# A four-layer convolution and scan kernel: the WKV layer's backward pass reordered and partly moved to PSUM, and the zero frames of layer 0 written in other shapes

## The chip, the core and the metric

The kernel runs on one core of one Trainium2 chip, as a single program of four layers. The metric is the device time of one execution in microseconds (us): the median of three runs. A profile of one further execution, with the hardware profiler, gives the times of single instructions. The engines are PE (TensorE: matrix products), DVE (VectorE), ACT (ScalarE), POOL (GpSimd) and SP, which here only issues DMAs. SBUF is the on-chip memory, PSUM the small memory with eight banks that PE writes its products to, and a DMA moves data between these and the DRAM.

## The reference

The input x has shape [2, 192, 96, 96]: two images, 192 channels, 9216 positions. Each layer normalizes its input and adds its result to it. Two of the four layers bear on the change.

Layer 0 is a convolution with learned offsets. A 1x1 product reduces 192 channels to 180 and another makes offsets; values are then gathered around each position with bilinear weights, and a position outside the image counts as zero.

Layer 2 is the WKV recurrence, over the 9216 positions in order, for each channel by itself. It has three products, k, v and r, of the normalized input, and then, as the reference writes it:

```
no = max(o, u + k);  A = exp(o - no);  B = exp(u + k - no)
y  = (A*p + B*v) / (A*q + B)
no2 = max(w + o, k); A2 = exp(w + o - no2); B2 = exp(k - no2)
p, q, o = A2*p + B2*v,  A2*q + B2,  no2
```

The recurrence runs over the positions in both directions, and the mean of the two results is taken; the kernel brings both quotients over one denominator, in which the sigmoid of r enters as a factor 1 + exp(-r). The product of mean and sigmoid is then normalized over the channels, multiplied by the matrix w_o and added to x.

## The kernel before, in words

**Layer 0.** DRAM holds two frames per image: xp_d, the reduced image with a border of zeros (PITCH = 106 rows and columns, of CW = 194 values), and o_d, the offsets, with zero rows ahead and behind. Before the reduce stage a tile of zeros is set by one DVE memset (L250), and six DMAs per image on ACT's queue write the borders (L256 to L273): two for o_d in 97 lanes, two for the full rows of xp_d in 106 lanes, two for its side strips in 96 lanes. A lane is one partition of the zero tile. The reduce stage (`reduce0`) then loads 128 positions at a time on SP's queue (L283), normalizes them on DVE (xn, L114), multiplies on PE (L300) and writes both frames through a tile xk (L294). Its tiles take memory that the zero tile had, so they wait for the zero DMAs to finish.

**Layer 2.** The two images' 192 channels each are packed in three groups g of 128 lanes: g = 0 and 1 hold the first 128 channels of each image, g = 2 the 64 that remain of both. The positions are cut into 18 chunks of 512. The loop runs over 54 chunk-groups forward and then over 54 backward. In this layer PE, ACT, DVE and POOL each execute in the order in which the program text issues (`manual_schedule`), so the order of the calls in the loop is the schedule. DMAs are issued by SP ahead of it.

An iteration i works on several chunk-groups at once:

- `key(i+3)`: matmuls for k into PSUM (L1607, two buffers).
- `carry(i+2)`: ACT copies the three columns in which the scans start from the previous tile of this group (L1708).
- `top(i+2)`: a DVE scan for the running maximum (L1719), and z = k minus it (L1728).
- `weighted(i+1)`: ACT makes four weights of z, each by Relu (L1734) and Exp (L1736).
- `times_v(i+1)` and `own(i)`: POOL multiplies weights by v (L1751, L1777).
- `value(i+2)` (forward): matmuls for v and an ACT copy with bias (L1685). `gate(i+1)` (backward): matmuls for r into the same PSUM buffer, and on ACT Relu (L1693) and Exp (L1694) into er, in SBUF with two buffers.
- `sums(i)`: two DVE scans (L1758) and two products (L1772) for numerator and denominator.
- `ended(i)`: two POOL sums (L1782, L1783). Forward, the result goes to DRAM as half_d; backward it is loaded again.
- Backward alone: `crossed(i-1)` (POOL, L1790) and `joined(i-1)` combine the two directions: three DVE operations (L1794, L1795, L1796, the last multiplying by 1 + er), a POOL sum (L1799), and on ACT Ln and Exp (L1801, L1802), which approximate an inverse r0. `inverse(i-2)` (POOL, L1807) and `scaled(i-2)` (DVE, L1814, L1817) do one Newton step and make h.

When the three groups of a chunk are done, a `tail` starts. It is a generator that is advanced twice per iteration: PE subtracts the channel mean (L1558, 16 matmuls), ACT squares (L1831), PE sums the squares (L1838), ACT takes the inverse root by Ln and Exp (L1840, L1841), DVE and POOL refine it by a Newton step (L1845, L1846, L1848), PE spreads it (L1852, `turn`), DVE multiplies h (L1853), PE multiplies by w_o (L1860, L1863) for each of two halves m, and DVE adds bias and input (L1873) and takes statistics (L1881). Two tails can be under way at once.

Of the kernel before, what the change touches and what calls it, by code (L numbers as in the profile page):

```python
# [61 lines left out]
class Net:  # L62
# [130 lines left out]
    def reduce_constants(self, wn, xp_d, o_d):  # L193
# [5 lines left out]
        with tc.tile_pool(name="wr0", bufs=1) as wr, tc.tile_pool(  # L199
# [49 lines left out]
            zero = wr.tile([PITCH, 8 * NS], F32, name="zero")  # L249
# [3 lines left out]
            for b in range(B):  # L253

                for lo, n in ((0, 2 * OB), (HW, OB + OA)):
                    nc.scalar.dma_start(  # L256
                        out=o_d[b][lo : lo + n].rearrange("(p r) c -> p (r c)", p=97),
                        in_=zero[:97, : n // 97 * 2 * NS],
                    )
                for lo, hi in ((0, F), (F + H, PITCH)):  # L260
                    rows = xp_d[b][lo:hi].rearrange("y x c -> (y x c)")
                    nc.scalar.dma_start(
                        out=rows.rearrange("(p f) -> p f", p=PITCH),
                        in_=zero[:, : (hi - lo) * CW],
                    )
                nc.scalar.dma_start(
                    out=xp_d[b][F : F + H, :F, :].rearrange("y x c -> y (x c)"),
                    in_=zero[:H, : F * CW],
                )
                nc.scalar.dma_start(  # L270
                    out=xp_d[b][F : F + H, F + W :, :].rearrange("y x c -> y (x c)"),
                    in_=zero[:H, : end * CW],
                )  # L273
# [1214 lines left out]
    def layer2(self, x, out, stats):  # L1488
# [10 lines left out]
        with ExitStack() as ctx:  # L1499
# [5 lines left out]
            pk = ctx.enter_context(tc.tile_pool(name="l2k", bufs=2, space=PSUM))  # L1505
            pv = ctx.enter_context(tc.tile_pool(name="l2v", bufs=1, space=PSUM))
            pa = ctx.enter_context(tc.tile_pool(name="l2a", bufs=2, space=PSUM))
            pm = ctx.enter_context(tc.tile_pool(name="l2m", bufs=3, space=PSUM))
# [29 lines left out]
            for g in range(3):  # L1538
                pt = pm.tile([P, T], F32, name="pm")
                nc.tensor.transpose(pt[:2, :P], mean[:, g], self.ident)  # L1540
                nc.vector.tensor_scalar(turn[:, g], pt[:2, :P], -0.5 * C, None, ALU.mult)
# [146 lines left out]
            def gate(i):  # L1688
                back, c, g = seq[i]
                pe = pv.tile([P, T], F32, name="v")  # L1690
                project(pe, g, lambda b: weights_of["r", b], lambda b, j: xts[back, c][b][:, j])
                er = sb.tile([P, T], F32, name="er")
                nc.scalar.activation(er, pe, AF.Relu, bias=bias["r"][:, g : g + 1])  # L1693
                nc.scalar.activation(er, er, AF.Exp, bias=far, scale=-1.0)  # L1694
                got[i]["er"] = er
# [92 lines left out]
            def crossed(i):  # L1788
                nd, half = got[i]["nd"], got[i]["half"]
                nc.gpsimd.tensor_tensor(half[:, 0], half[:, 0], nd[:, 1], ALU.mult)  # L1790

            def joined(i):
                nd, half = got[i]["nd"], got[i]["half"]
                nc.vector.tensor_tensor(nd[:, 0], nd[:, 0], half[:, 1], ALU.mult)  # L1794
                nc.vector.tensor_tensor(nd[:, 1], nd[:, 1], half[:, 1], ALU.mult)  # L1795
                nc.vector.scalar_tensor_tensor(  # L1796
                    nd[:, 1], got[i]["er"], 1.0, nd[:, 1], ALU.add, ALU.mult
                )
                nc.gpsimd.tensor_tensor(nd[:, 0], nd[:, 0], half[:, 0], ALU.add)  # L1799
                r0 = sb.tile([P, T], F32, name="r0")  # L1800
# [3 lines left out]

            def inverse(i):
                nd = got[i]["nd"]
                nc.gpsimd.tensor_tensor(nd[:, 1], nd[:, 1], got[i]["r0"], ALU.mult)  # L1807

            def scaled(i):
                back, c, g = seq[i]  # L1810
                nd, r0 = got[i]["nd"], got[i]["r0"]
                if g == 0:
                    chunks[c] = s3.tile([P, 3, T], F32, name="h")
                nc.vector.scalar_tensor_tensor(  # L1814
# [6 lines left out]
            def tail(c):  # L1821
# [17 lines left out]
                r0 = s1.tile([2, T], F32, name="rs0")  # L1839
                nc.scalar.activation(r0, pt[:2], AF.Ln, bias=self.eps[:2])  # L1840
                nc.scalar.activation(r0, r0, AF.Exp, scale=-0.5)  # L1841
                yield
                yield
                rs = s1.tile([2, T], F32, name="rs")
                nc.vector.scalar_tensor_tensor(rs, pt[:2], EPS, r0, ALU.add, ALU.mult)  # L1845
                nc.gpsimd.tensor_tensor(rs, rs, r0, ALU.mult)  # L1846
                yield
                nc.vector.scalar_tensor_tensor(rs, rs, -3.0, r0, ALU.add, ALU.mult)  # L1848
# [45 lines left out]
            def back(i):  # L1894
                return 0 <= i < n and seq[i][0]
# [3 lines left out]
            for i in range(3):  # L1899
                key(i)  # L1900
            for i in range(2):
                carry(i)
                value(i)
                top(i)
            weighted(0)
            times_v(0)
            tails = []
            for i in range(n + 9):
                at(load, i + 6)
                at(load_half, i + 2)  # L1910
                at(key, i + 3)
                at(carry, i + 2)
# [4 lines left out]
                if back(i - 2):  # L1917
                    inverse(i - 2)
# [3 lines left out]
                at(times_v, i + 1)  # L1922
                if i + 2 < n and not back(i + 2):
                    value(i + 2)
                if back(i + 1):
                    gate(i + 1)
                if i < n:
                    sums(i)
                at(top, i + 2)
                if i < n:  # L1930
                    ended(i)
                if back(i - 1):
                    joined(i - 1)
                if back(i - 2):
                    scaled(i - 2)
# [545 lines left out]
```

## Time and profile before

| quantity | value |
|---|---|
| median of 3 runs | 10991.94 us (10980.75 to 10996.88) |
| profiled execution: own time, span | 11003.03 us, 11001.3 us |
| granted clock of TensorE, mean | 0.889 |
| busy over the span: PE, DVE, ACT, POOL | 87%, 78%, 54%, 65% |
| layer 0; layer 1 | 0 to about 5930 us; to about 6266 us |
| layer 2, forward half | 6266 to 6621 us: PE 245, DVE 312, ACT 310, POOL 266 us busy, clock 0.93 |
| layer 2, backward half | 6621 to 7666 us: PE 796, DVE 782, ACT 464, POOL 567 us busy, clock 0.67 |
| layer 3 | 7666 us to the end |

How to read the profile: a row of a timeline gives start, duration, engine, line, operation, output <- inputs, and in brackets how long the engine was idle before it, and what released it. A row of a group gives the line, the operation with its tiles, a count, then busy time and mean duration in ns, then idle time ahead of it. A row of waits gives the total in us, how often, and the longest. PE's clock runs at full or at half rate; 0.67 is a mean over time. The shares over the whole span mix four layers and say little on a single one.

### The profile page before, as it was taken

The numbers are of one execution on the slowest core, as the hardware profiler recorded it, in microseconds if no ns is written. First come the engines' busy times: TensorE is split into PE (matmuls) and PEld (weight loads), VectorE is DVE, ScalarE is ACT, GpSimd is POOL, SyncE is SP. The second block draws the span as 40 slices with busy tenths as digits, with TensorE's granted clock in tenths as the row PEclk, the third lists the DMA queues.
The fourth block names the chain that finished last, engine by engine and source line by source line (L and its number), as shares of the span: only waits on it lengthen the run. The fifth ranks groups of instructions, "written<-read, shape, count | busy, mean of one in ns | idle before, by whom it ended". The sixth has DMA issues, their size and how long they took to land.

```text
span 11001.3 us, 230434 instructions
## 1 busy us (share of the span) xinstructions
PE 9621.3 (87%) x92621; PEld 5592.7 (51%) x92621; DVE 8540.5 (78%) x8810; ACT 5977.8 (54%) x11192; POOL 7104.0 (65%) x5527
## 2 busy tenths in 40 slices
PE   2799999999899999999567667777899999999998
PEld 1588888888788888888422222222222222222222
DVE  3677777777677777777556798776599999999999
ACT  0266666666576666667200095443466666666664
POOL 0366676767556666666311386553688888988888
PEclk9999999999999999999788696666788888888887
DMA  6433333333233333333343253222577777777776
GB/s 113 99 91 95 96 97 95 99 94 98 65 80 92 91 90 94 89 92 89 102 122 107 82 181 100 81 86 61 122 172 171 172 171 172 173 170 171 173 170 148
DMA packets 601618, 1282.73 MB, mean 117 GB/s; under 512 B 238592, under 2 KB 321780, under 8 KB 544224
## 3 DMA queue, kind: packets, MB, share of 16 engines
q1 hardware_dynamic: 387560, 1081.12, 39.5%
q0 software_dynamic: 103808, 133.18, 5.1%
q10 hardware_dynamic: 109176, 53.57, 1.8%
q8 instruction: 739, 12.11, 0.5%
q14 instruction: 335, 2.74, 0.1%
HBM read 786.57 MB, written 231.25 MB: 93 GB/s over the span
## 4 chain that ended last, share of the span: by engine, by line
PE 23%; DVE 16%; ACT 6%; issue 4%; POOL 1%; DMA 0%; SPq 0%; DVEq 0%; ACTq 0%; POOLq 0%
DVE h L2223 6%; PE da L2199 5%; PE pe L2091 4%; PE pm L1558 3%; PE pe L2111 2%; ACT da L2213 2%; PE pe L1395 2%; PE acc L2270 2%; DVE hc L2246 2%; PE pe L2126 1%; ACT t L1734 1%; PE pe L1387 1%; PE acc L2264 1%; DVE nd L1796 1%; POOL ud L1445 1%
## 5 line engine op out<-in xcount | busy, mean ns | idle before, releaser
L569 DVE TENSOR_TENSOR sp<-h 128x2304 f32<-128x2304 f32 x790 | 2165.6, 2774 | 24.7 <-ACT h L548 24.7
L2223 DVE TENSOR_TENSOR_SCAN h<-da,state,bu 128x512 f32<-128x512 f32 x1632 | 1960.5, 1265 | 238.1 <-ACT da L2213 232.0
L2190 POOL TENSOR_TENSOR bu<-bu,bs 128x2048 f32<-128x2048 f32 x432 | 1955.8, 4527 | 16.8 <-DMA bu<-ud 16.8
L593 ACT COPY st<-pt 128x512 f32<-128x512 f32 (+1 forms) x2370 | 1217.6, 516 | 1312.3 <-PE pt L585 1243.2
L591 DVE COPY st<-pt 128x512 f32<-128x512 f32 x1580 | 1061.9, 687 | 976.5 <-PE pt L585 961.4
L585 PE MATMUL pt<-ident,sp 128*128 128x128 f32 x14220 | 1680.4, 276 | 98.2 <-DVE sp L569 57.2
L539 POOL TENSOR_TENSOR h<-u,step 128x1152 f32<-128x1152 f32 (+1 forms) x474 | 1199.4, 2544 | 821.3 <-DVE u L512 463.2
L585 PEld LDWEIGHTS pt<-ident,sp 128*128 128x128 f32 x14220 | 1566.7, 142 | 185.7 <-issue 92.1
L557 POOL DMA_DIRECT2D xw<-xp_d x2500 | 1389.6, 633 | 142.8 <-PE pt L632 82.4
L2213 ACT ACTIVATE da<-da,nA 128x512 f32<-128x512 f32 x1728 | 1047.5, 661 | 658.9 <-PE da L2199 657.7
L632 PE MATMUL pt<-st,xw 64*32 64x288 f32 (+1 forms) x30000 | 1073.1, 366 | 72.5 <-ACT st L593 28.6
L653 ACT COPY val<-pt 128x288 f32<-128x288 f32 (+1 forms) x3132 | 985.3, 398 | 207.5 <-PE pt L632 203.3
L2199 PE MATMUL da<-dl,spread 32*128 32x512 f32 x3456 | 985.7, 693 | 14.6 <-DVE h L2223 6.8
L700 PE MATMUL pf<-more,wl 54*64 54x128 f32 (+1 forms) x17064 | 955.2, 268 | 11.2 <-DMA more<-val 10.1
L700 PE MATMUL pf<-main,wd 126*64 126x128 f32 (+1 forms) x17064 | 962.1, 270 | 1.0 <-DMA main<-val 0.4
L700 PEld LDWEIGHTS pf<-main,wd 126*64 126x64 f32 x17064 | 889.7, 137 | 140.8 <-issue 133.2
L700 PEld LDWEIGHTS pf<-more,wl 54*64 54x64 f32 x17064 | 917.7, 135 | 47.4 <-issue 34.7
L632 PEld LDWEIGHTS pt<-st,xw 64*32 64x32 f32 x30000 | 540.1, 106 | 477.9 <-ACT val L653 173.2
L2246 DVE TENSOR_TENSOR hc<-h,cc 128x1536 f32<-128x1536 f32 x432 | 748.5, 1733 | 0.0
L2091 PE MATMUL pe<-xn,sb_w_in 96*128 96x512 f32 x864 | 572.2, 797 | 112.6 <-ACT xi L2099 63.2
L2257 POOL TENSOR_TENSOR hp<-h,cs 128x512 f32<-128x512 f32 x432 | 551.9, 1278 | 165.0 <-PE da L2199 97.3
L2199 PEld LDWEIGHTS da<-dl,spread 32*128 32x128 f32 x3456 | 301.5, 193 | 666.7 <-DVE h L2223 431.8
(344 smaller groups left out, 13505.1 us busy)
## 6 DMA issues: line engine op xcount, KB each, us to landing
bu<-ud SPq DMA_DIRECT2D x432, 1024.0 KB
main<-val SPq DMA_DIRECT2D x2016, 81.0 KB
more<-val SPq DMA_DIRECT2D x1728, 40.5 KB
xw<-xp_d POOLq DMA_DIRECT2D x2500, 26.0 KB
xt<-x_d SPq DMA_DIRECT2D x108, 384.0 KB
half_d<-hv SPq DMA_DIRECT2D x54, 768.0 KB
hv<-half_d SPq DMA_DIRECT2D x54, 768.0 KB
u_d<-u SPq DMA_DIRECT2D x158, 180.0 KB
```

Of the source, the lines that this page charges most:

```text
L539: nc.gpsimd.tensor_tensor(hs, u[:, :, 8 * KK * l : 8 * KK * l + n].unsqueeze(3).to_broadcast([P, 2, n, WS]), con["step"].unsqueeze(1).unsq ...
L557: nc.gpsimd.dma_start(out=xw[e * WN : (e + 1) * WN, i], in_=xp_d[y : y + WS, x : x + WS, e * CM // 2 : e * CM // 2 + XW],)
L569: nc.vector.tensor_tensor(sp.rearrange("p s (y x) -> p s y x", x=WS), hy.unsqueeze(3).to_broadcast([P, n, WS, WS]), hx.unsqueeze(2).to_bro ...
L585: nc.tensor.transpose(pt[:, q], sp[:, 2 * (q0 + q) : 2 * (q0 + q) + 2].rearrange("p e w -> p (e w)"), self.ident,)
L591: nc.vector.tensor_copy(st[:, q0 : q0 + m], pt[:, :m])
L593: nc.scalar.copy(st[:, q0 : q0 + m], pt[:, :m])
L632: nc.tensor.matmul(pvs[e][lane : lane + 32, j * w : (j + 1) * w], xw[e * WN : (e + 1) * WN, win, g * CG : g * CG + 32], sts[pair][e * WN : ...
L700: nc.tensor.matmul(to, wt[:, m * CO : (m + 1) * CO], took.rearrange("p h (r c) -> p h r c", c=columns), start=first and l == 0 and t == 0, ...
L2190: nc.gpsimd.tensor_tensor(bu, bu, got[s]["bs"].unsqueeze(1).to_broadcast([P, 4, T]), ALU.mult)
L2199: nc.tensor.matmul(das[r], spread[at, v].rearrange("p n e -> p (n e)"), got[s]["dl"][at, i], start=True, stop=True, tile_position=(32 * r, 0),
L2213: nc.scalar.activation(da, da, AF.Exp, scale=nA[:, 4 * q + r : 4 * q + r + 1])
L2223: nc.vector.tensor_tensor_scan(h[:, r], got[s]["da", q][r], bu[:, r], init, ALU.mult, ALU.add)
```

## The change

In layer 0, the zero tile becomes 96 lanes of 5141 columns (`part`). The full rows of xp_d are written in 16 and 24 lanes and come first; o_d is written in 48 and 96 lanes; the side strips stay as they are.

In layer 2, the PSUM banks are divided differently: k has one buffer instead of two, v two instead of one, the shared tile pm two instead of three, and r0 gets one of its own. `gate` writes er over its own PSUM tile, and r0 is in PSUM. `crossed` takes over the product that L1795 did on DVE, on POOL. `inverse` is gone as a step of its own; its product is now on DVE at the head of `scaled`. In `joined` the operation with er comes first. In the tail the Newton step of the root is gone, with its two pauses and L1845 to L1848, and `turn` has another factor accordingly. In the loop, `carry(i+3)` stands directly behind `sums(i)`, `gate` and `scaled` stand behind that, `key(i+3)` moves behind `top(i+2)`.

```diff
-            zero = wr.tile([PITCH, 8 * NS], F32, name="zero")
+            part = PITCH * CW // 4
+            zero = wr.tile([CH, part], F32, name="zero")
...
-                for lo, n in ((0, 2 * OB), (HW, OB + OA)):
-                    nc.scalar.dma_start(
-                        out=o_d[b][lo : lo + n].rearrange("(p r) c -> p (r c)", p=97),
-                        in_=zero[:97, : n // 97 * 2 * NS],
-                    )
                 for lo, hi in ((0, F), (F + H, PITCH)):
                     rows = xp_d[b][lo:hi].rearrange("y x c -> (y x c)")
                     nc.scalar.dma_start(
-                        out=rows.rearrange("(p f) -> p f", p=PITCH),
-                        in_=zero[:, : (hi - lo) * CW],
+                        out=rows.rearrange("(p f) -> p f", f=part), in_=zero[: 4 * (hi - lo)]
+                    )
+                for lo, n in ((0, 2 * OB), (HW, OB + OA)):
+                    most = 2 * OB * 2 * NS // (CH // 2)
+                    nc.scalar.dma_start(
+                        out=o_d[b][lo : lo + n].rearrange("r c -> (r c)").rearrange(
+                            "(p f) -> p f", f=most
+                        ),
+                        in_=zero[: n * 2 * NS // most, :most],
                     )
...
-            pk = ctx.enter_context(tc.tile_pool(name="l2k", bufs=2, space=PSUM))
-            pv = ctx.enter_context(tc.tile_pool(name="l2v", bufs=1, space=PSUM))
+            pk = ctx.enter_context(tc.tile_pool(name="l2k", bufs=1, space=PSUM))
+            pv = ctx.enter_context(tc.tile_pool(name="l2v", bufs=2, space=PSUM))
             pa = ctx.enter_context(tc.tile_pool(name="l2a", bufs=2, space=PSUM))
-            pm = ctx.enter_context(tc.tile_pool(name="l2m", bufs=3, space=PSUM))
+            pr = ctx.enter_context(tc.tile_pool(name="l2r", bufs=1, space=PSUM))
+            pm = ctx.enter_context(tc.tile_pool(name="l2m", bufs=2, space=PSUM))
...
-                nc.vector.tensor_scalar(turn[:, g], pt[:2, :P], -0.5 * C, None, ALU.mult)
+                nc.vector.tensor_scalar(turn[:, g], pt[:2, :P], float(C), None, ALU.mult)
...
-                er = sb.tile([P, T], F32, name="er")
-                nc.scalar.activation(er, pe, AF.Relu, bias=bias["r"][:, g : g + 1])
-                nc.scalar.activation(er, er, AF.Exp, bias=far, scale=-1.0)
-                got[i]["er"] = er
+                nc.scalar.activation(pe, pe, AF.Relu, bias=bias["r"][:, g : g + 1])
+                nc.scalar.activation(pe, pe, AF.Exp, bias=far, scale=-1.0)
+                got[i]["er"] = pe
...
                 nc.gpsimd.tensor_tensor(half[:, 0], half[:, 0], nd[:, 1], ALU.mult)
+                nc.gpsimd.tensor_tensor(nd[:, 1], nd[:, 1], half[:, 1], ALU.mult)
...
-                nc.vector.tensor_tensor(nd[:, 0], nd[:, 0], half[:, 1], ALU.mult)
-                nc.vector.tensor_tensor(nd[:, 1], nd[:, 1], half[:, 1], ALU.mult)
                 nc.vector.scalar_tensor_tensor(
                     nd[:, 1], got[i]["er"], 1.0, nd[:, 1], ALU.add, ALU.mult
                 )
+                nc.vector.tensor_tensor(nd[:, 0], nd[:, 0], half[:, 1], ALU.mult)
                 nc.gpsimd.tensor_tensor(nd[:, 0], nd[:, 0], half[:, 0], ALU.add)
-                r0 = sb.tile([P, T], F32, name="r0")
+                r0 = pr.tile([P, T], F32, name="r0")
...
-            def inverse(i):
-                nd = got[i]["nd"]
-                nc.gpsimd.tensor_tensor(nd[:, 1], nd[:, 1], got[i]["r0"], ALU.mult)
...
+                nc.vector.tensor_tensor(nd[:, 1], nd[:, 1], r0, ALU.mult)
                 nc.vector.scalar_tensor_tensor(
                     r0, nd[:, 1], -2.0, r0, ALU.add, ALU.mult
                 )
...
-                r0 = s1.tile([2, T], F32, name="rs0")
-                nc.scalar.activation(r0, pt[:2], AF.Ln, bias=self.eps[:2])
-                nc.scalar.activation(r0, r0, AF.Exp, scale=-0.5)
+                rs = s1.tile([2, T], F32, name="rs")
+                nc.scalar.activation(rs, pt[:2], AF.Ln, bias=self.eps[:2])
+                nc.scalar.activation(rs, rs, AF.Exp, scale=-0.5)
                 yield
-                yield
-                rs = s1.tile([2, T], F32, name="rs")
-                nc.vector.scalar_tensor_tensor(rs, pt[:2], EPS, r0, ALU.add, ALU.mult)
-                nc.gpsimd.tensor_tensor(rs, rs, r0, ALU.mult)
-                yield
-                nc.vector.scalar_tensor_tensor(rs, rs, -3.0, r0, ALU.add, ALU.mult)
                 yield
...
-                at(key, i + 3)
-                at(carry, i + 2)
                 for t in tails:
                     next(t, None)
                 if back(i - 1):
                     crossed(i - 1)
-                if back(i - 2):
-                    inverse(i - 2)
                 if i < n:
                     own(i)
                 at(weighted, i + 1)
                 at(times_v, i + 1)
+                if i < n:
+                    sums(i)
+                at(carry, i + 3)
                 if i + 2 < n and not back(i + 2):
                     value(i + 2)
                 if back(i + 1):
                     gate(i + 1)
-                if i < n:
-                    sums(i)
+                if back(i - 2):
+                    scaled(i - 2)
                 at(top, i + 2)
+                at(key, i + 3)
                 if i < n:
                     ended(i)
                 if back(i - 1):
                     joined(i - 1)
-                if back(i - 2):
-                    scaled(i - 2)
                 for t in tails:
                     next(t, None)
```

More of the change, by code (lines that the diff above doesn't have):

```diff
@@ L1898, in layer2 @@
                 at(load, i)
-            for i in range(3):
-                key(i)
             for i in range(2):
                 carry(i)
+                key(i)
                 value(i)
                 top(i)
+            key(2)
+            carry(2)
             weighted(0)
```

## The prediction

> **What bounds the kernel now.** The change touches two stages of one long serial program: the zero writes at the start of layer 0, and layer 2. I read first the busy time by stretches, then the waits, the timeline and the groups of instructions inside each stretch.
>
> Layer 0 starts with a hole. Waits and stretches (columns of a stretch: length, then busy PE, PEld, DVE, ACT, POOL, granted clock, DMA share, GB/s):
>
> ```profile
> L250 DVE MEMSET zero<- x1: 1258/1258/1258, 50.7 to 50.7; 106x1440 f32 x1
> POOL xk L294 <- DMA xp_d<-zero: 98.8, 1, 98.8
> 100.00:110.00 10.00, 0.00 (x0) 0.00 (x0) 0.00 (x0) 0.00 (x0) 0.00 (x0) 1.00 0.06 25
> 210.00:220.00 10.00, 4.15 (x9) 3.18 (x10) 3.57 (x14) 0.00 (x0) 0.32 (x2) 0.50 0.93 200
> ```
>
> From 85 to 161 us nothing computes. The first xk, and the first loads of x into buffers that take the zeros' place, wait for the zeros: they are issued from 52.0 us, and the first normalize (xn, L114) starts at 162.6. While they flow, DMA is busy for 0.06, one engine of 16, at 25 GB/s.
>
> Layer 2 runs from 6266 to 7666 us. The forward half is bound by ACT, 310 of 355 us, without gaps once it runs. The backward half is my second subject (6621 to 7666). From 6726 to 7545 it repeats every 57.2 us, one chunk of three group-iterations: L1853, the last step of a tail, starts its three at 6726.40, 6783.57 and 6840.91. Waits, then the timeline of one chunk:
>
> ```profile
> DVE opq L1719 <- ACT opq L1708: 175.9, 15, 11.7
> ACT er L1693 <- DVE nd L1796: 134.0, 52, 4.4
> ...
> 6727.14 2.08 PE L1558 MATMUL pm<-h,center 128*128 128x512 f32 x2 [6.38 <-DVE h L1853]
> 6742.85 0.60 ACT L1831 ACTIVATE sq<-pm 128x512 f32<-128x512 f32 x1 [6.99 <-PE pm L1558]
> 6743.34 0.19 ACT L1708 COPY opq<-opq 128x3 f32<-128x3 f32 x1
> 6743.56 1.28 DVE L1719 TENSOR_TENSOR_SCAN opq<-w,opq,k 128x512 f32<-128x512 f32 x1 [11.73 <-ACT opq L1708]
> 6772.46 5.48 PE L1852 MATMUL pm<-rs,turn 2*128 2x512 f32 x6 [3.86 <-DVE rs L1848]
> ```
>
> Once per chunk a three-column copy (L1708) stands on ACT behind the squares of a tail; these wait for the 16 centering matmuls (15.7 us at half clock), and DVE idles 11.73 us. Otherwise DVE sets the pace: 43.4 busy of 57.
>
> **Zeros: -79 us.** The transfers carry about 4.75 MB over both images: per image 818 KB of o_d, 803 KB of full rows of xp_d and 728 KB of side strips. Today 97- and 106-lane transfers carry two thirds of it. The trace says one engine gives 25 GB/s. The Trainium skill ("DMA: Bandwidth & Descriptors", section on why a DMA increments its semaphore by 16) says that a DMA uses the largest number of engines up to 16 that divides both slowest dimensions: 97 gives 1, 106 gives 2, 24 gives 12, and 16, 48 and 96 give 16. The rows at 25 GB/s agree with the first. By that rule, 16 times 25 GB/s moves 4.75 MB in 12 us; by the best row nearby (200 GB/s) it takes 24. The memset grows with its columns, 1.26 x 5141/1440 = 4.5 us, so zeros start near 55 and land between 70 and 81. Small DVE constants (about 36 us of operations of 0.15 to 0.19) now interleave with the first normalizes; some 20 stand ahead, 3.5 us. First xn at 76 to 85, against 162.6: 78 to 87 gained, less up to 10 for the constants that used to lie under the wait. Bounds -60 to -88; I take -79.
>
> **Forward half: +8.** No operation goes. key(i+3) moves directly behind value's matmuls, so that PE has one gap of 1.9 us per 5.83 us iteration instead of two. The clock flips here on a grid of 3.41 us, as the rows show:
>
> ```profile
> 6762.51:6765.93 3.42, 1.69 (x8) 0.50 (x5) 3.35 (x5) 1.29 (x2) 1.45 (x1) 1.00 0.32 69
> 6765.93:6769.34 3.41, 2.67 (x4) 0.58 (x2) 3.18 (x5) 3.22 (x7) 0.01 (x1) 0.50 0.90 318
> ```
>
> A stretch busy 0.49 is followed by half clock; stretches at 0.57 were not. The worst forward stretch falls from 0.57 to about 0.43, so half clock can come. A key then takes 3.5 us, inside the 3.85 us before its scan, so ACT stays the bound: 0 to +30, I take +8.
>
> **Backward half, what goes.** (a) The copy of carried columns stands behind its own scans, ahead of any squares: the 11.73 us stall ends. (b) Newton steps leave the tail: L1848's 1.79, L1845's 0.66 and a 1.43 wait on POOL, and PE waits less for turn. (c) er and r0 in PSUM. The groups show why this matters to DVE:
>
> ```profile
> L1796 DVE SCALAR_TENSOR_TENSOR nd<-er,nd 128x512 f32<-128x512 f32 x54 | 88.3, 1636 | 1.9
> L1772 DVE TENSOR_TENSOR nd<-e,opq 128x512 f32<-128x512 f32 x108 | 67.9, 669 | 0.0
> L1814 DVE SCALAR_TENSOR_TENSOR r<-nd,r 128x512 f32<-128x512 f32 x53 | 75.5, 1425 | 0.0
> ```
>
> With all operands in SBUF, beside POOL, an operation takes 1.4 to 1.6; with one operand in PSUM (e) 0.67. L1796 saves 0.95, L1814 0.7, L1817 0.33; L1795 (1.08) moves to POOL, and POOL's inverse (1.54) becomes a DVE operation of 0.7. DVE per group: sums 3.86, three scaled operations 2.05, top 1.96, the operation on er 0.68; 8.55 of durations, 8.2 by starts, as neighbours overlap. POOL has seven operations of 1.27, 8.9: close behind, not ahead.
>
> **Backward half, what comes.** er now lives in gate's PSUM tile, which has two buffers. So gate(i+1) on PE waits until joined(i-1) has read er, late in the same iteration. Before, ACT took this wait (the er row above, 134 us in 52 waits), with PE's gate already done. Queued behind gate on PE are key(i+3) and then the tail's matmuls; on DVE the tail's own operations stand directly behind joined and wait for those. On ACT the Relu and Exp, Ln and Exp, squares and the next weights wait as well, and POOL's bv behind these. So in each of the three iterations DVE now waits for gate + key + the tail's matmuls. Rows of PE:
>
> ```profile
> 6742.74 3.78 PE L1607 MATMUL k<-xt,wk 96*128 96x512 f32 x4
> 6754.81 1.98 PE L1607 MATMUL k<-xt,wk 96*128 96x512 f32 x4
> 6749.30 1.88 PE L1860 MATMUL pm<-h,wo 128*96 128x512 f32 x4
> ```
>
> Per chunk, from the end of joined's operation: A (gate, key, wo of half 0), B (the same for half 1), C (gate, key, turn). Full clock: A and B 2.0 + 2.0 + 1.9 + 1.1, less overlaps, then 2.8 of DVE (two of L1873 and L1881 each): 9.3. C: 3.9, first turns, 1.8 of DVE: 7.4. Sum with 3 x 8.2: 50.7 us. Half clock: A and B 3.8 + 3.4 + 5.4, then 2.8: 15. C 3.4 + 3.4 + 5.5 and the last multiply: 13.4. Sum 68.
>
> Which clock holds? The trace: half clock came after a stretch busy 0.49, rises took 4.3 to 7.1 us from the start of full key or gate matmuls, and 13.65 us of centering, 13.65 busy, stayed at 0.50. In the new order PE idles about 8 us ahead of A and of C, while the 8.2 us of a group pass on DVE and release nothing to it. A then runs cold through gate, key and most of wo: 13.5. B follows A's centering after about 2 us: 11. C is cold: 12.9. Sum 37.4 + 24.7 = 62.1.
>
> The Trainium skill ("TensorE: Matmul & The Clock Gate", Part 1) makes it otherwise: full clock after about one busy window of 3.4 us, half after an idle one. A would be warm after some 5 us, the centering behind it also, B all warm, C warm for turn: about 54.2 us per chunk. The centering at 0.50 contradicts it here, so I take 62.3 between the two ends 50.7 and 68, near the trace's reading. Against 57.2 that is +5.1 in each of (7545 - 6648)/57.2 = 15.7 periods: **+80**, range +55 to +105 in this case. The first five iterations, without tails: 12.0 each before, about 11.0 after: -5. In the last tails (7545 to 7666) two Newton chains of about 7 us each are exposed and go: -13.
>
> **Sum.** -79 + 8 - 5 + 80 - 13 = -9. The profiled execution took 11003.03 us (span 11001.3), above the median 10991.94. Against the median: **10983**. Measurements can tell 0.2%, 22 us, from no change.
>
> **Rivals.**
> - *PE gets warm.* If gate and key at the head of A lift the clock, as the Skill has it, a chunk costs 50.7 to 56, 1 to 6 us less than before: -19 to -102 in layer 2, 10800 to 10885 in all. For it: key and gate at 6754 to 6763 ran warm directly behind each other. Against: idle stretches ahead of A and C.
> - *PE stays cold, slower.* One mechanism: gate's wait. If the clock stays low through A, B and C, or the centering (15.7 us cold) has not ended when B's gate is free, a chunk takes 66 to 73: 15.7 x 9 to 16 = +140 to +250; with the other terms -89, 11040 to 11150. It decides from a chunk of 57.2 + (89 + 22)/15.7 = 64.3 us on. For it: mean clock 0.67 already; against: wo and key warmed within a chunk before.
> - *The zeros' gain does not reach the end.* Reduce may wait then for its constants, or for the 10112 small pieces of at_d, which occupied the engines 22 us. Zeros worth -30: 11030.
> - *Forward becomes bound by PE*: at half clock 6.8 to 7.0 per iteration, +50 to +66: 11035.
> - *Nothing in the wait changes*: if er's wait costs as little as on ACT, a chunk falls to DVE's 34 to 45 us; excluded by PE's order, where gate stands ahead of the tail's matmuls.
>
> **Numbers.** Half clock in A and C (10950 to 11020): 0.50, of which 0.16 under 10970, 0.24 within, 0.10 over 11014. Warm: 0.18, all faster. Cold: 0.20, slower. Zeros lost 0.05, slower 0.03, within 0.02. Forward 0.07, slower 0.06, within 0.01. Faster 0.34, same 0.27, slower 0.39. Range 10870 to 11095: it leaves out the deepest warm and the coldest cases.
>
> **What would show it.** First xn at 76 to 85 us, with DMA over 150 GB/s before. No DVE wait on L1708's copy. L1796's successor near 0.68. A wait of PE's gate on DVE's joined in nearly every backward iteration; DVE waits on PE in A, B and C; L1853 repeating at about 62 us, and clock 0.5 to 0.6 in the backward half. A period under 56 or over 65 makes the prediction wrong, as does a forward half longer by over 30.

## The result

The changed kernel takes 11011.18 us (median of 20 runs, 11004.85 to 11021.74) against 10988.81 (20 runs, 10968.0 to 10999.93): a ratio of 1.0022, 95% interval 1.0015 to 1.0029. It is slower by 22 us, and the interval excludes that nothing changed. The forecast was 10983, a gain of 9.

The two profiled executions differ by less, 11003.03 and 11009.99 us (spans 11001.3 and 11008.2), since that of before lay 14 us above its median. The sum by stages is made between these two, so it accounts for 7 of the 22 us. Its marks are the starts of the DVE scan of the running maximum (L1719 before, L1721 after): the 1st, the 55th (first of the backward half), the 63rd (where tails begin) and the 108th, the last.

| stage | before, us | after, us | difference | forecast |
|---|---|---|---|---|
| start to 1st scan (zeros) | 6272.76 | 6198.52 | -74.2 | -79 |
| forward half | 340.94 | 332.33 | -8.6 | +8 |
| backward, without tails | 78.44 | 77.70 | -0.7 | -5 |
| backward, 15 chunks with tails | 852.13 (56.8 each) | 962.23 (64.15 each) | +110.1 | +80 |
| last tails, then layer 3 | 3457.0 | 3437.4 | -19.6 | -13 |
| sum | 11001.3 | 11008.2 | +7.0 | -9 |

The last row's difference lies in the last tails: from the last scan to the last addition of the tails (L1873, after L1866) it is 122.6 us before and 103.2 after, and layer 3 behind it takes the same time within 0.3 us.

Each step of the prediction can be read in the trace of after. First the start of layer 0: the memset of the zero tile, the longest wait for its transfers, one stretch (columns: length, busy PE, PEld, DVE, ACT, POOL, clock, DMA share, GB/s), and the operation of DVE that they release:

```profile
L251 DVE MEMSET zero<- x1: 4343/4343/4343, 55.7 to 55.7; 96x5141 f32 x1
POOL lane L355 <- DMA xp_d<-zero: 33.2, 1, 33.2
75.00:85.00 10.00, 0.00 (x0) 0.00 (x0) 0.00 (x0) 0.00 (x0) 0.00 (x0) 1.00 0.72 180
87.53 0.06 DVE L368 MEMSET at<- 128x1 f32 x1 [16.51 <-DMA xp_d<-zero]
```

The memset took 4.34 us (4.5 forecast) but ended at 60.0 instead of 55. In the stretch shown the zeros flowed at 180 GB/s with DMA 0.72 busy, and DVE was released at 87.5, some 27 us after the first of them was issued. The first normalize started at 91.1 us, against 162.6. That is later than the 76 to 85 of the forecast: of its two rates, 200 GB/s (24 us) was nearer than 16 times 25 GB/s (12 us), an estimate that takes the number of engines from the Trainium skill ("DMA: Bandwidth & Descriptors", the section on why a DMA increments its semaphore by 16) and the 25 GB/s from the trace of before.

Then the waits of the backward half, and the group of the scan that stalled before:

```profile
DVE yo L1866 <- PE pm L1856: 320.8, 35, 15.2
PE v L1610 <- DVE nd L1797: 309.4, 51, 9.2
DVE h L1846 <- PE pm L1845: 178.0, 54, 8.9
```

```profile
L1721 DVE TENSOR_TENSOR_SCAN opq<-w,opq,k 128x512 f32<-128x512 f32 x93 | 118.5, 1274 | 0.4 <-PE k L1610 0.2
L1813 DVE SCALAR_TENSOR_TENSOR r<-nd,r 128x512 f32<-128x512 f32 x51 | 35.5, 696 | 1.8
L1797 DVE SCALAR_TENSOR_TENSOR nd<-v,nd 128x512 f32<-128x512 f32 x52 | 35.4, 681 | 0.7 <-POOL nd L1793 0.7
```

The stall behind the carried columns, 175.9 us before, is gone. The operations with an operand in PSUM take 0.68 to 0.70 us, as forecast. In their place stand two waits that feed each other: PE's gate waits for DVE's joined (L1797) in nearly every iteration, 309 us, and DVE waits for the tail's matmuls, 321 + 178 us. One chunk on PE, and the waits of DVE in it:

```profile
6843.07 3.78 PE L1610 MATMUL v<-xt,wr 96*128 96x512 f32 x4 [8.96 <-DVE nd L1797]
6846.78 3.69 PE L1610 MATMUL k<-xt,wk 96*64 96x512 f32 x8
6850.40 2.42 PE L1853 MATMUL pm<-h,wo 128*96 128x512 f32 x4
6854.69 1.12 PE L1561 MATMUL pm<-h,center 128*128 128x512 f32 x2 [0.83 <-DVE yo L1866]
...
6865.06 3.75 PE L1610 MATMUL v<-xt,wr 96*128 96x512 f32 x4 [2.08 <-DVE nd L1797]
...
6885.96 3.69 PE L1610 MATMUL v<-xt,wr 96*64 96x512 f32 x8 [7.54 <-DVE nd L1797]
```

```profile
6853.89 0.75 DVE L1866 SCALAR_TENSOR_TENSOR yo<-pm,bo,yo 96x512 f32<-96x512 f32 x1 [10.27 <-PE pm L1856]
6874.88 0.75 DVE L1866 SCALAR_TENSOR_TENSOR yo<-pm,bo,yo 96x512 f32<-96x512 f32 x1 [9.38 <-PE pm L1856]
6895.40 0.69 DVE L1846 TENSOR_TENSOR h<-h,pm 128x512 f32<-128x512 f32 x1 [8.89 <-PE pm L1845]
```

These are A, B and C of the prediction. From the end of joined's operation on er (L1797) to the start of the next group's first scan they took 13.6, 12.7 and 13.5 us; forecast were 13.5, 11 and 12.9. Only B was well off: it ran at half clock although PE had been idle for just 2.08 us ahead of it. The stretches of the clock's grid show why:

```profile
6861.57:6864.98 3.41, 1.41 (x3) 0.19 (x2) 3.26 (x6) 1.93 (x4) 0.02 (x1) 1.00 0.00 0
6864.98:6868.39 3.41, 3.33 (x4) 1.51 (x5) 0.53 (x1) 3.25 (x6) 3.41 (x3) 0.51 0.00 0
6868.39:6871.80 3.41, 3.41 (x5) 1.29 (x4) 0.00 (x0) 2.88 (x6) 3.33 (x4) 0.50 0.10 18
6871.80:6875.22 3.42, 3.05 (x9) 0.73 (x7) 0.34 (x1) 0.00 (x0) 2.29 (x2) 0.99 0.59 212
```

The gap fell into one stretch, in which PE was busy for 1.41 of 3.41 us; half clock followed for two stretches of almost unbroken work (3.33 and 3.41 us busy), and full clock in the next.

### The profile page after: what moved, and what is told of

It reads as the page before. It is cut to its first block, busy times and chain, and to the rows that moved or that the text cites. A ratio compares the mean times of both kernels' runs of the same rounds, so it can differ in the third digit from the quotient of the medians.

```text
span 11008.2 us, 230320 instructions
## 1 busy us (share of the span) xinstructions
PE 9637.1 (88%) x92621; PEld 5615.5 (51%) x92621; DVE 8353.8 (76%) x8774; ACT 5975.1 (54%) x11192; POOL 7016.4 (64%) x5509
## 4 chain that ended last, share of the span: by engine, by line
PE 26%; DVE 16%; ACT 5%; issue 3%; POOL 1%; DMA 0%; SPq 0%; DVEq 0%; ACTq 0%; POOLq 0%
DVE h L2215 6%; PE da L2191 5%; PE pe L2083 4%; PE pe L2103 2%; ACT da L2205 2%; PE pe L1397 2%; PE acc L2262 2%; PE v L1610 2%; DVE hc L2238 2%; PE k L1610 1%; PE pe L2118 1%; PE pe L1389 1%; DVE opq L1760 1%; PE pm L1845 1%; PE acc L2256 1%
## 5 line engine op out<-in xcount | busy, mean ns | idle before, releaser
L2083 PE MATMUL pe<-xn,sb_w_in 96*128 96x512 f32 x864 | 572.2, 797 | 112.8 <-ACT xi L2091 63.3
```

## The experiments

Each run is compared with the kernel before in the same series; the ratios are to it. "A chunk" is three group-iterations of the backward half, the mean of 15 as in the table above.

**The two parts apart.** First the kernel before with only the zero writes changed:

```diff
-            zero = wr.tile([PITCH, 8 * NS], F32, name="zero")
+            part = PITCH * CW // 4
+            zero = wr.tile([CH, part], F32, name="zero")
...
-                        out=rows.rearrange("(p f) -> p f", p=PITCH),
-                        in_=zero[:, : (hi - lo) * CW],
+                        out=rows.rearrange("(p f) -> p f", f=part), in_=zero[: 4 * (hi - lo)]
```

> The kernel before, with the new shapes of the zero writes alone. Theory: the first normalize starts near 91 us instead of 163, and the 74 us gained there reach the end untouched: about 10915 us. Rival: the reduce stage gives a part back later, since its own loads and constants are then late: 10950 us or more.

Measured: 10931.77 us against 11003.04, ratio 0.9937 (0.9920 to 0.9953), -71 us. The gain of the first 90 us reaches the end.

Then the change of layer 2 alone, with the zeros as before:

```diff
-            pv = ctx.enter_context(tc.tile_pool(name="l2v", bufs=1, space=PSUM))
+            pv = ctx.enter_context(tc.tile_pool(name="l2v", bufs=2, space=PSUM))
...
-                got[i]["er"] = er
+                got[i]["er"] = pe
...
-                at(key, i + 3)
-                at(carry, i + 2)
...
+                at(carry, i + 3)
...
+                at(key, i + 3)
```

> The kernel before, with the change of layer 2 alone. Theory: layer 2 loses about 81 us between the two traces, and the two parts add up: 11070 to 11085 us, a backward chunk of 64 us. Rival: part of the loss comes from the earlier start (the clock's grid falls otherwise), and layer 2 alone loses less than 50: under 11040 us.

Measured: 11085.59 us, ratio 1.0079 (1.0062 to 1.0095), +83 us, a chunk of 64.13 us. The parts add up to +11 us, between the +7 of the profiled pair and the +22 of the medians; each ratio is known to about 0.16%, 18 us, so that the sum does not decide between them. Both theories stand: zeros gain, layer 2 loses more.

**gate's wait.** er is put back to SBUF; everything else stays as in the changed kernel. gate's PSUM tile is then free as soon as ACT has read it.

```diff
-                nc.scalar.activation(pe, pe, AF.Relu, bias=bias["r"][:, g : g + 1])
-                nc.scalar.activation(pe, pe, AF.Exp, bias=far, scale=-1.0)
-                got[i]["er"] = pe
+                er = sb.tile([P, T], F32, name="er")
+                nc.scalar.activation(er, pe, AF.Relu, bias=bias["r"][:, g : g + 1])
+                nc.scalar.activation(er, er, AF.Exp, bias=far, scale=-1.0)
+                got[i]["er"] = er
```

> The changed kernel, with er in SBUF again (two buffers) while gate keeps its two PSUM buffers, so that gate no longer waits on PE for joined. Theory (gate's wait on PE holds the tail's matmuls up): only key and the tail's matmuls are left between joined and the tail's DVE work, 3.5 us less in each of A, B and C, and the operation on er costs 0.5 to 0.9 us more: a chunk of 54 to 57 us, 10850 to 10900 us. Rival (the tail's order itself, or PE's clock, and not the wait): a chunk of 62 us or more, 10980 us or more.

Measured: 10814.56 us, ratio 0.9828 (0.9812 to 0.9845), a chunk of 51.31 us. This is 12.8 us less per chunk than in the changed kernel: one buffer decided the sign of the whole change. It was more than forecast. The trace shows two reasons: the operation on er did not get dearer (0.681 us, as in PSUM; POOL idles at that time, waiting for it or for the product behind it), and gate, now early, stands in PE's idle stretch. What waits now is key, and gate of B runs at full clock:

```profile
6831.91 1.94 PE L1610 MATMUL v<-xt,wr 96*64 96x512 f32 x8
6838.93 3.78 PE L1610 MATMUL k<-xt,wk 96*128 96x512 f32 x4 [5.07 <-DVE z L1731]
...
6873.21 1.98 PE L1610 MATMUL v<-xt,wr 96*128 96x512 f32 x4
6875.03 1.88 PE L1610 MATMUL k<-xt,wk 96*128 96x512 f32 x4
```

gate (v) follows the work before it at once; key, with its single buffer, waits 5.07 us for z. The last two rows are gate and key of B: behind the same centering, but with no idle time ahead of them, they take 3.5 us together, where the changed kernel takes 6.9 behind its gap of 2.08 us.

**key's wait too.** k gets two buffers again, and v one, as in the kernel before:

```diff
-            pk = ctx.enter_context(tc.tile_pool(name="l2k", bufs=1, space=PSUM))
-            pv = ctx.enter_context(tc.tile_pool(name="l2v", bufs=2, space=PSUM))
+            pk = ctx.enter_context(tc.tile_pool(name="l2k", bufs=2, space=PSUM))
+            pv = ctx.enter_context(tc.tile_pool(name="l2v", bufs=1, space=PSUM))
```

> er in SBUF as in the run before, and the PSUM buffers of k and v as in the kernel before (k two, v one), so that key no longer waits for z either. Theory (what stands between joined and the tail's DVE work sets the chunk): only the tail's matmuls are left there, a chunk of 45 to 48 us against 51.3, 10740 to 10770 us. Rival: PE, idle for longer, drops to half clock more often and becomes the bound (57 us of work per chunk at half clock): 51 us or more, 10810 us or more.

Measured: 10663.82 us, ratio 0.9694 (0.9678 to 0.9710), a chunk of 41.33 us: 334 us faster than before, with two edits to the changed kernel, and 4 us per chunk better than expected. Of the tail's waits on DVE little is left, and gate and key run behind each other, at full clock in two of the three iterations:

```profile
6853.54 0.75 DVE L1867 SCALAR_TENSOR_TENSOR yo<-pm,bo,yo 96x512 f32<-96x512 f32 x1 [1.64 <-PE pm L1857]
6869.05 0.74 DVE L1867 SCALAR_TENSOR_TENSOR yo<-pm,bo,yo 96x512 f32<-96x512 f32 x1 [3.88 <-PE pm L1857]
6883.43 0.69 DVE L1847 TENSOR_TENSOR h<-h,pm 128x512 f32<-128x512 f32 x1 [1.57 <-PE pm L1846]
```

10.27, 9.38 and 8.89 us in the changed kernel are here 1.64, 3.88 and 1.57. The rival, a PE that gets colder by waiting, went the other way: the mean clock of 6700 to 7300 us rose from 0.68 to 0.82.

**r0 in PSUM.** The changed kernel with er and r0 both in SBUF, to be set against the run with er alone there:

```diff
-                r0 = pr.tile([P, T], F32, name="r0")
+                r0 = sb.tile([P, T], F32, name="r0")
```

> The changed kernel with er and also r0 in SBUF. Theory (an operation of DVE with all operands in SBUF takes 1.4 us and more beside POOL, 0.69 with one in PSUM): the three operations of scaled run beside POOL's sums and cost together 1.4 to 2.1 us more per group, a chunk of 55 to 57 us against 51.3, 10870 to 10900 us. Rival (POOL waits at that time, and they do not meet): 51 to 52 us, 10815 to 10830 us.

Measured: 10868.10 us, ratio 0.9884 (0.9868 to 0.9901), a chunk of 55.03 us, 3.7 more than with r0 in PSUM. The three operations of scaled, in this run:

```profile
L1813 DVE SCALAR_TENSOR_TENSOR r<-nd,r 128x512 f32<-128x512 f32 x33 | 43.7, 1325 | 1.1
L1816 DVE SCALAR_TENSOR_TENSOR h<-nd,r 128x512 f32<-128x512 f32 x33 | 32.4, 983 | 3.6
L1812 DVE TENSOR_TENSOR nd<-nd,r 128x512 f32<-128x512 f32 x33 | 30.1, 914 | 0.0
```

Against 0.70, 0.69 and 0.68 us they cost together 1.16 us more per group, 3.5 per chunk, which is nearly the whole difference. The theory holds; the 1.4 to 2.1 us expected were too much, while the prediction's 0.7 and 0.33 for the first two of these were near the 0.63 and 0.30 measured.

**Which of the two waits.** The counterpart: r0 in SBUF, k in two buffers, er in PSUM, so that gate waits and key has its buffer free.

```diff
-            pk = ctx.enter_context(tc.tile_pool(name="l2k", bufs=1, space=PSUM))
+            pk = ctx.enter_context(tc.tile_pool(name="l2k", bufs=2, space=PSUM))
...
-                r0 = pr.tile([P, T], F32, name="r0")
+                r0 = sb.tile([P, T], F32, name="r0")
```

> The changed kernel with r0 in SBUF and k in two buffers: gate still waits on PE for joined, key no longer for z. The counterpart, where key waits and gate does not, had a chunk of 55.0 us. Theory (either wait puts four matmuls between joined and the tail's, so they cost alike): 55 to 59 us, 10870 to 10930 us. Rival (gate's wait is the dearer, because ACT, too, stands behind it): 61 to 65 us, 10960 to 11020 us.

Measured: 11077.56 us, ratio 1.0074 (1.0057 to 1.0091), a chunk of 68.10 us. Both expectations missed. 68.1 is the changed kernel's 64.15 and the 3.7 us that r0 in SBUF cost, so that key's second buffer seems to have brought nothing (no run has r0 alone in SBUF). In the trace key waits for nothing of its own, but stands behind gate on PE:

```profile
6844.82 3.69 PE L1609 MATMUL v<-xt,wr 96*64 96x512 f32 x8 [9.36 <-DVE nd L1796]
6848.43 3.78 PE L1609 MATMUL k<-xt,wk 96*128 96x512 f32 x4
```

So the waits are not alike. Taking gate's away gave 12.8 us per chunk (64.15 less 51.3). Taking key's away, with v at one buffer, gave 10.0 (51.3 less 41.3), and that only once gate's was gone.

**The tail's matmuls in front.** If the wait costs by what is queued behind it, those matmuls can go in front of it. w_o and the first two of the three turns are issued half an iteration ahead of the DVE operations that read them; the third turn has to wait for one of pm's two buffers:

```diff
                 yield
-                yield
+                turned = []
                 for g in range(3):
+                    if g == 2:
+                        yield
+                        nc.vector.tensor_tensor(h[:, 0], h[:, 0], turned[0], ALU.mult)
                     pt = pm.tile([P, T], F32, name="pm")
                     nc.tensor.matmul(pt, turn[:, g], rs, start=True, stop=True)
-                    nc.vector.tensor_tensor(h[:, g], h[:, g], pt, ALU.mult)
+                    turned.append(pt)
+                for g in (1, 2):
+                    nc.vector.tensor_tensor(h[:, g], h[:, g], turned[g], ALU.mult)
                 yield
                 for m in range(2):
-                    yield
...
+                    yield
                     for b in range(B):
                         yo = yos[b]
```

On the changed kernel, where gate still waits:

> The changed kernel with its buffers and its waits of gate and key as they are, and the tail's matmuls of turn and w_o issued half an iteration ahead, in front of gate. Theory (the wait costs by what is queued behind it): with the tail's matmuls in front, a chunk of 36 to 43 us against 64, 10590 to 10700 us. Rival (the loop joined, gate, ACT, joined is a bound by itself): 50 us or more, 10800 us or more.

Measured: 10921.87 us, ratio 0.9936 (0.9919 to 0.9952), a chunk of 57.73 us. The direction is right, the size is not. The number is in the rival's range, but its mechanism is not seen: one iteration of three takes 11.53 us with gate waiting in it, so the loop through gate and ACT does not hold a chunk to 50 us. The other two iterations lose the time elsewhere:

```profile
6839.99 2.08 PE L1561 MATMUL pm<-h,center 128*128 128x512 f32 x2
...
6855.59 3.73 PE L1857 MATMUL pm<-h,wo 128*96 128x512 f32 x4
```

```profile
6823.74 0.69 DVE L1851 TENSOR_TENSOR h<-h,pm 128x512 f32<-128x512 f32 x1 [7.29 <-PE pm L1848]
6861.23 0.75 DVE L1871 SCALAR_TENSOR_TENSOR yo<-pm,bo,yo 96x512 f32<-96x512 f32 x1 [16.49 <-PE pm L1860]
```

In one, the third turn still stands behind gate and key, and DVE waits 7.29 us for it. In the other, the centering matmuls now run at half clock, 15.6 us instead of 8.3, and w_o of the other half stands behind them on PE; DVE waits 16.49 us for it.

The same edit on the kernel with er in SBUF and k in two buffers:

> The kernel with er in SBUF and k two, v one, with the tail's matmuls of turn and w_o issued half an iteration ahead of the DVE operations that read them, so in front of gate and key on PE. Theory (DVE's remaining waits are for the tail's matmuls): they go, a chunk of 35 to 38 us against 41.3, 10580 to 10620 us. Rival: another engine is the bound by then (PE by its clock, ACT or POOL), 40 us or more, 10640 us or more.

Measured: 10661.43 us, ratio 0.9699 (0.9683 to 0.9715), a chunk of 42.4 us, no gain over 41.3. Both numbers are in the rival's range:

```profile
6700.00:7200.00 500.00, 467.61 (x886) 123.93 (x885) 410.21 (x515) 293.66 (x505) 307.97 (x242) 0.78 0.36 108
```

PE is busy 468 of 500 us at a clock of 0.78, so that PE by its clock is the likely bound. In four of the 15 chunks one iteration takes 20 to 22 us instead of 12; in the one from 6877.87 us on, the centering runs at half clock.

**The clock.** Matmuls that nobody reads are added to the changed kernel, to fill PE's idle stretch ahead of A and C; eight of them first:

```diff
                 for t in tails:
                     next(t, None)
+                if tails and i < n and i % 3 != 2:
+                    pt = pm.tile([P, T], F32, name="pm")
+                    for _ in range(2):
+                        project(
+                            pt,
+                            0,
+                            lambda b: weights_of["k", b],
+                            lambda b, j: xts[seq[i][0], seq[i][1]][b][:, j],
+                        )
```

> The changed kernel, with eight matmuls more behind the tail's in the iterations ahead of A and of C, whose product nobody reads; they fill the stretch in which PE waits for joined. Theory (half clock after that idle stretch is what makes A and C long): gate and key run in 2 us each instead of 3.7, A near 9.5, C near 8, B 9.5 to 12.5, a chunk of 52 to 56 us, 10830 to 10890 us. Rival (the wait alone counts, whatever the clock, or PE stays at half clock): a chunk of 64 us or more, 11010 to 11100 us.

Measured: 10993.32 us, ratio 0.9992 (0.9983 to 1.0001), a chunk of 63.30 us. The filler ended 2.4 to 3.9 us ahead of gate, which still ran mostly at half clock (3.46 and 3.69 us). Neither range was met, and by itself this decides nothing: either the clock has another cause, or a gap of that length is enough. So twelve:

```diff
-                    for _ in range(2):
+                    for _ in range(3):
```

> The changed kernel with twelve matmuls to fill the idle stretch of PE instead of eight; eight ended 2 to 4 us ahead of gate, and gate still ran at half clock. Theory (it is the idle stretch just ahead of gate that puts it to half clock): gate and key in 2 us each, a chunk of 53 to 58 us, 10840 to 10920 us. Rival (the clock falls for another reason, or the filler holds gate up): 62 us or more, 10980 us or more.

Measured: 10899.95 us, ratio 0.9912 (0.9895 to 0.9928), a chunk of 57.89 us. Work that is of no use made the changed kernel 1.1% faster (0.9912 against 1.0022).

```profile
6842.24 2.05 PE L1610 MATMUL v<-xt,wr 96*128 96x512 f32 x4 [1.99 <-DVE nd L1797]
6844.09 3.55 PE L1610 MATMUL k<-xt,wk 96*128 96x512 f32 x4
...
6861.50 3.69 PE L1610 MATMUL v<-xt,wr 96*64 96x512 f32 x8 [2.19 <-DVE nd L1797]
```

The theory is borne out in part: gate now runs at full clock in some places (2.05 us), but the 2 us left idle still bring half clock just behind or ahead of it. The mean clock of 6700 to 7300 us rose from 0.68 to 0.84. If the filler acts by the clock alone, which no run separates, half clock is worth at least 6 us per chunk of the changed kernel. What the chunk would be with no half clock at all was not measured.

**Parts of the change alone, on the kernel before.** The carried columns copied directly behind their scans:

```diff
-                at(carry, i + 2)
...
                 if i < n:
                     sums(i)
+                at(carry, i + 3)
```

> The kernel before, with the copy of the carried columns directly behind its own scans, and nothing else of the change. Theory: DVE's stall of 11.73 us per chunk goes, and about half of it is handed to the tail's chain: a chunk of 50 to 53 us, 10915 to 10950 us. Rival: the tail's chain of centering, root and turn sets the period, and the stall moves to it whole: 56 us or more, over 10980 us.

Measured: 10987.15 us, ratio 0.9991 (0.9982 to 1.0000), a chunk of 55.3 us. The stall of 11.73 us went, and another came, nearly as large as the rival said:

```profile
6866.06 0.75 DVE L1873 SCALAR_TENSOR_TENSOR yo<-pm,bo,yo 96x512 f32<-96x512 f32 x1 [14.33 <-PE pm L1863]
```

The same centering, from 6841.88 to 6857.5 us at half clock, with key and gate behind it, now stops DVE at the tail's addition instead of at the scan.

And the root without its Newton step, and so without its two pauses; turn gets the other factor here too:

```diff
                 yield
-                yield
-                rs = s1.tile([2, T], F32, name="rs")
-                nc.vector.scalar_tensor_tensor(rs, pt[:2], EPS, r0, ALU.add, ALU.mult)
-                nc.gpsimd.tensor_tensor(rs, rs, r0, ALU.mult)
-                yield
-                nc.vector.scalar_tensor_tensor(rs, rs, -3.0, r0, ALU.add, ALU.mult)
                 yield
```

> The kernel before with the root's Newton step gone and nothing else of the change. Theory (by the rows, 2.45 us of DVE and 1.43 us of waiting per chunk, and turn no longer waits for them): a chunk of 51 to 54 us against 57.2, 10895 to 10950 us. Rival: the carried columns' stall takes it back, 56 us or more, over 10970 us.

Measured: 10838.95 us, ratio 0.9857 (0.9841 to 0.9874), a chunk of 48.87 us: 153 us, by far the best single part, and twice what its rows add up to. turn no longer waits for the root's last step, nor PE for turn, and the centering starts earlier:

```profile
6852.17 2.84 PE L1846 MATMUL pm<-rs,turn 2*128 2x512 f32 x6
6865.57 1.12 PE L1558 MATMUL pm<-h,center 128*128 128x512 f32 x2
6866.63 1.12 PE L1558 MATMUL pm<-h,less 64*128 64x512 f32 x2
6873.49 2.08 PE L1558 MATMUL pm<-h,center 128*128 128x512 f32 x2 [5.74 <-DVE yo L1867]
```

turn runs at full clock in 2.84 us, where it took 5.48 behind an idle stretch of 3.86, and a quarter of the centering is done before PE has to wait. The stall at the scan is 6.83 us where it was 11.73. Without its pauses the tail is also one iteration shorter; how much of the gain is due to the operations and how much to the pauses was not separated.

All runs, in us. The kernel before had medians of 10988.81 to 11003.04 in the four series, so that ratios compare better than times:

| kernel | chunk | time | ratio |
|---|---|---|---|
| before | 56.8 | 10988.81 | 1 |
| changed | 64.15 | 11011.18 | 1.0022 |
| zeros alone | 56.8 | 10931.77 | 0.9937 |
| layer 2 alone | 64.1 | 11085.59 | 1.0079 |
| changed, er in SBUF | 51.3 | 10814.56 | 0.9828 |
| changed, er in SBUF, k two, v one | 41.3 | 10663.82 | 0.9694 |
| the same, tail's matmuls in front | 42.4 | 10661.43 | 0.9699 |
| changed, er and r0 in SBUF | 55.0 | 10868.10 | 0.9884 |
| changed, r0 in SBUF, k two | 68.1 | 11077.56 | 1.0074 |
| changed, tail's matmuls in front | 57.7 | 10921.87 | 0.9936 |
| changed, filler of 8 / of 12 | 63.3 / 57.9 | 10993.32 / 10899.95 | 0.9992 / 0.9912 |
| before, carry moved | 55.3 | 10987.15 | 0.9991 |
| before, no Newton step | 48.9 | 10838.95 | 0.9857 |

## Why the prediction was wrong

The time lay inside the range and inside the likeliest case (10950 to 11020), but the sign was wrong: -9 was forecast, +22 measured. Its own chances had slower (0.39) slightly ahead of faster (0.34).

*The step that failed* is the cost of a chunk in "Backward half, what comes", and in it the clock of B. "B follows A's centering after about 2 us: 11" was 12.7. The centering ran at full clock as assumed, but the 2.08 us of idle time behind it were enough to lose it: gate and key of B took 6.9 us, where they take 3.5 with no gap (er in SBUF). C was 13.5 for 12.9, A and the three groups were right within 0.3 us. The chunk was 64.15 for 62.3, and before it was 56.8 and not 57.2 over the whole stretch: +7.3 us a chunk against +5.1, and +110 for the stretch against +80. These 30 us are more than the forecast gain of 9; B alone makes 1.7 us of a chunk, 26 over 15 chunks.

*Luck.* In the traces the forward half and the last tails came out 23 us better than forecast and hid most of these 30 (the zeros and the iterations without tails were 9 worse), so that the total of the traces is +7. The other 15 of the 22 us lie between the medians and the profiled executions, and no stage accounts for them. The prediction's own point of decision, a chunk of 64.3 us, was met almost exactly, but with -103 us from the other stages instead of the -89 that it rests on.

*The two readings of the clock.* In B half clock followed a stretch busy for 0.41, and full clock came 6.7 us after work began. The other reading, 54.2 us a chunk by the Trainium skill ("TensorE: Matmul & The Clock Gate", Part 1: half clock after at least one idle window, full clock after a busy one of about 3.4 us), was the farther one. The mean clock did not fall to the 0.5 to 0.6 that was to show the mechanism: it was 0.68 from 6700 to 7300 us, for 0.67 before.

*gate's wait: right, and the heart of it.* That er in PSUM makes PE wait for joined, with key and the tail's matmuls behind it and DVE behind these, was read from the program and is what the trace shows. Taking that one wait away gave 12.8 us per chunk.

*What goes: right in the rows, wrong in what they are worth.* The stall at the scan, the contended operations and the Newton step all went as forecast. But they were no separate gains. The carried columns alone were worth 1.5 us of their 11.73; the Newton step alone 8 us where its rows gave 3.9. That fits a chain of a tail, with its centering at half clock, as what bound the kernel before, and not the place where DVE happened to stand; what that chain would take at full clock was not tested. And the 0.95 us saved on the operation on er were not owed to PSUM: in the new order it took 0.681 us with er in SBUF as well. For r0 the place did count, 1.16 us per group.

*Zeros: nearly right.* -74 in the traces and -71 alone, for -79. Starting time and rate were both a little too good. (The shares that the prediction lists, 2349 KB per image, make 4.81 MB and not 4.75, which moves nothing.)

*Forward half: wrong sign, small.* +8 forecast, -8.6 measured. The iteration stayed at 5.83 us although the clock fell from 0.93 to 0.82, as said. The gain is in the first two iterations, 19.38 and 19.25 us before, 17.86 and 12.04 after. The change also reorders the calls ahead of the loop:

```diff
-            for i in range(3):
-                key(i)
             for i in range(2):
                 carry(i)
+                key(i)
                 value(i)
                 top(i)
+            key(2)
+            carry(2)
```

With it the first matmuls of v start 3 us ahead of the first scan (6195.49 us); before, they stood behind three keys and started 23 us after it (6296.02). The prediction had not costed this start. No run has it alone.

*The other rivals.* PE did not stay cold through the centering, and the zeros' gain was not lost. "Nothing in the wait changes" was excluded because gate stands ahead of the tail's matmuls; with er in SBUF and two buffers for k, 41 us was within the 34 to 45 named there.

## What to carry to other kernels

When a result is kept in the PSUM tile that a matmul wrote, the next matmul into that buffer waits for the last reader, and everything behind it on PE waits along: look up who reads last and what is queued behind before saving an SBUF operand. Where an engine stalls, ask what chain releases it: moving the stalled instruction out of the way gave 1.5 us of 11.73 here, while shortening the chain by one small step gave 8 us, twice what its rows say. And the price of a wait on PE is not only its length: in B the 2.08 us without work were followed by 6.9 us of gate and key at half clock, 3.4 us more than without the gap.

## What the runs showed of the hardware

- PE work added without use shortened the time: twelve filler matmuls per idle stretch took the changed kernel from a ratio of 1.0022 to 0.9912, and its chunk from 64.15 to 57.89 us.
- An idle gap shorter than the grid's 3.41 us was enough for half clock, where it left one stretch of the grid busy for 0.41; full clock came back only after two stretches busy for 0.98 and 1.00 (6861.57 to 6871.80 us of the changed kernel).
- The centering matmuls did not raise the clock by themselves. Where they started at half clock they stayed there for 15.6 us of uninterrupted work (changed kernel with the tail's matmuls in front; the kernel before); where they started at full clock they took 8.3 us. In the kernel before, 62 stretches of the grid between 6500 and 7700 us are filled by them alone at half clock, and none is followed by full clock. Why is open; 12 of the 16 use 64 of the rows or columns.
- What an operation of DVE takes beside POOL depended on the moment and not on the place of the operand alone: the operation on er, in SBUF, took 1.64 us before, 0.681 in the new order, where POOL waits for it, and 1.00 where the tail's matmuls were in front.
